# Layer 3 of a four-layer graph kernel: other tile shapes on TensorE, the key turn read from SBUF, and a new planned order

## The chip, the cores and the metric

The kernel runs on one core of a Trainium2 chip. The metric is the device time of one execution in microseconds; the kernel before is given as the median of three runs. A core has five engines that work side by side: TensorE (PE, matrix products; its weight loads are shown apart as PEld), VectorE (DVE), ScalarE (ACT), GpSimd (POOL) and SyncE (SP, which only issues DMAs). Matrix products land in PSUM, which ACT and DVE read; everything else lives in SBUF.

## The reference

Sixteen graphs (B = 16) of N = 1024 nodes with 128 features and a 0/1 adjacency matrix go through four layers. Each layer's result is added to its input, and a layer norm follows. Cut to what matters here:

```python
# layer 0: one head of additive attention, relu
# layer 1: eight heads of additive attention with 16 columns each, elu
# layer 2: mean over neighbours, product with a weight matrix, layer norm, relu
def _L3_gnn_ref(features, adj_matrix, W):               # layer 3
    D = W.shape[-1]                                     # 4 heads, D = 32
    Wh = jnp.einsum('bsf,hfd->bhsd', features, W)
    scores = jnp.einsum('bhsd,bhtd->bhst', Wh, Wh) / jnp.sqrt(jnp.float32(D))
    scores = jnp.where(adj_matrix[:, None, :, :] > 0, scores, NEG_INF)
    attn = jax.nn.softmax(scores, axis=-1)
    h = jnp.einsum('bhst,bhtd->bhsd', attn, Wh)
    ...
x = _layernorm(x + _L0_gnn_ref(x, adj, ...), axis=-1)
x = _layernorm(x + _L1_gnn_ref(x, adj, adj, ...), axis=-1)
x = _layernorm(x + _L2_gnn_ref(x, adj, ...), axis=-1)
x = _layernorm(x + _L3_gnn_ref(x, adj, ...), axis=-1)
```

## The kernel before

The kernel does not write its instructions in program order. It describes every graph as a list of steps, and a planner (class `Plan`) decides the order in which they are issued. A step has an engine, an estimated cost in microseconds, a due time, the buffers it reads and writes, and a function that issues its instructions. The planner keeps a clock for each engine from these estimates; among the open steps that could start first on an engine it takes the one with the earliest due time, and only those due within `AHEAD` of the oldest unfinished step. `LAG` and `SLACK` are added to the time at which a result counts as ready. `SWITCH` is added to a PE step whose `mode` differs from the one before. Each engine then runs its own list strictly in that order, and semaphores carry the dependences. So an estimate or a due time changes nothing by itself; it changes the order.

Buffers come from named pools. PSUM has two `wk` tiles of 128 x 1024 (two banks each), two `acc1` tiles and two `acc3` tiles of 128 x 512. SBUF pools bear on it too: nine `z` tiles (layer 1's weights), four `z3` tiles (layer 3's weights), six `gap` tiles, seven `R` tiles, and `m`, the adjacency in one byte, for three graphs.

The steps that matter, by graph:

- Layer 0 (`layer0`): DVE makes weights at L622, PE sums them at L634 into `acc1`.
- Layer 1 (`layer1`): for two groups of four heads and eight blocks j of 128 nodes, DVE makes four weight tiles of 128 x 1024 at L774, and PE sums them at L782, as two steps of four matmuls with 32 columns each, into `acc1`. The sums of weights come from a column of ones that stands in `hh1` beside each head's 16 values. ACT copies out at L812.
- Layer 2 (`layer2`): PE products with the adjacency at L914.
- Before layer 3 (`before3`), for each of two chunks of 512 nodes: transposes, the product with W at L991 into one half of a `wk` tile, a copy to `whT` at L995, the turn of the keys by seven small ACT copies at L1004 and L1006 (so that head h's 32 rows meet the right columns), transposes of the result into the other half of the same `wk` tile, and a copy to `hh` at L1018.
- Layer 3 (`layer3`), for two halves of 512 query nodes and eight blocks j of key nodes: ACT makes `gap` (L1060), zero at an edge and one elsewhere. One PE step makes the scores of all four heads in both `wk` tiles: at L1070 sixteen bf16 matmuls in 32x32 tiles put a large negative number where there is no edge, and at L1080 four fp32 matmuls, one for each head's 32 rows and 128 columns, add the products. ACT takes the exp of each `wk` tile into `z3` (L1113). Two PE steps at L1092 sum the weights into `acc3`, with two matmuls of 64 columns each: 32 values, one column of ones, and 31 zeros. `LATER3` sets how much later than the scores these steps are due.

Layer norms run on ACT (L426, L454), with small DVE steps and a power on POOL (L442). Due times come from the calls at the end of the function, once for each graph, `PERIOD` apart; graphs overlap, so that one graph's layer 1 stands beside the layer 3 of the graph before it.

The SP queue issues the loads of `x`, `xT` and `R` and the stores; POOL's queue issues the loads of `m` between its powers and reductions.

Of the kernel before, what the change touches and what calls it, by code (L numbers as in the profile page):

```python
# [76 lines left out]
class Plan:  # L77
# [6 lines left out]
    SLACK = 0.00  # L84
    SWITCH = 0.1
    SAME = 0.0
    AHEAD = 327.0

    def __init__(self):
        self.steps = []  # L90
        self.places = {}
        self.users = {}
        self.turns = {}

# [8 lines left out]
    def step(self, engine, us, due, emit, reads=(), writes=(), lag=None, holds=(), floor=0.0, mode="full"):  # L103
        s = Step(engine, us, due, emit, self.LAG if lag is None else lag, mode)
        s.ready = floor
        for buf in holds:
            s.bufs.append(buf)
            buf.left += 1
        follows = set()
        for keys, writing in ((reads, False), (writes, True)):  # L110
            for key in keys:
                buf, part = key if isinstance(key, tuple) else (key, None)
                if buf not in s.bufs:
                    s.bufs.append(buf)
                    buf.left += 1
                buf.parts.setdefault(part, [None, []])
                for p, (writer, readers) in buf.parts.items():
                    if part is None or p is None or p == part:
                        if writer:
                            follows.add(writer)  # L120
                        if writing:
                            follows.update(readers)
        for keys, writing in ((reads, False), (writes, True)):
            for key in keys:
                buf, part = key if isinstance(key, tuple) else (key, None)
                if writing:
                    for p in list(buf.parts):
                        if part is None or p == part:
                            buf.parts[p] = [s, []]
                else:  # L130
                    buf.parts[part][1].append(s)
        follows.discard(s)
        s.waits = len(follows)
        for f in follows:
            f.next.append(s)
        self.steps.append(s)
        return s
# [83 lines left out]
def tile_binary(  # L221
# [32 lines left out]
    W3 = D3 + 1  # L254
    F8 = mybir.dt.float8e5
    PAD1 = 32 - W1
    PAD3 = 64 - W3
# [14 lines left out]
    nc.gpsimd.memset(neg_half, -0.5)  # L272
    neg_one = const.tile([P, 1], F32, name="neg_one")
# [13 lines left out]
    LATER1 = 3.4  # L287
    LATER3 = 13.7
# [27 lines left out]

    plan.pool("wk", wks)
# [25 lines left out]
    for t in places("hh3", 3, [P, HB, H3 * W3 + PAD3]):  # L343
        nc.vector.memset(t[:, :, : H3 * W3].rearrange("p k (h c) -> p k h c", c=W3)[:, :, :, D3:], 1.0)
        nc.vector.memset(t[:, :, H3 * W3 :], 0.0)
# [191 lines left out]
    def before0(b, due):  # L537
# [11 lines left out]
        for chunk in range(2):  # L549
# [8 lines left out]
            ps, view = products(xT, w0c, due, hd, 0.93)  # L558
# [121 lines left out]
    def before1(b, due):  # L680
# [8 lines left out]
        for chunk in range(2):  # L689
            ks = slice(chunk * HB, (chunk + 1) * HB)  # L690
            xT = turned(x1, chunk, due + chunk)
            ps, view = products(xT, w1c, due + chunk, hh, 1.0)
# [169 lines left out]
    def layer2(b, due):  # L862
# [7 lines left out]
        for chunk in range(2):  # L870
            ks = slice(chunk * HB, (chunk + 1) * HB)
            xT = turned(x2, chunk, due + chunk)
            ps, view = products(xT, w2c, due + chunk, y2, 1.76)
# [101 lines left out]
    def before3(b, due):  # L975
# [6 lines left out]

        def heads(hh):
            return hh.t[:, :, : H3 * W3].rearrange("p k (h c) -> p k h c", c=W3)[:, :, :, :D3]

        for chunk in range(2):
# [5 lines left out]
                [xT, w3c], [(ps, 0)], holds=[hh, whT, turn],  # L992
# [3 lines left out]
                [(ps, 0)], [whT],  # L996
            )

            def turned_groups(turn=turn, ps=ps):
                for h in range(H3):  # L1000
                    rows_h = slice(h * D3, (h + 1) * D3)
                    into = blocks_of(turn.t[rows_h, :])
                    of = blocks_of(ps.t[rows_h, :HALF])
                    nc.scalar.copy(into[:, :, h * D3 :], of[:, :, : P - h * D3])  # L1004
                    if h:
                        nc.scalar.copy(into[:, :, : h * D3], of[:, :, P - h * D3 :])  # L1006

            step("ACT", 2.6, due + chunk, turned_groups, [(ps, 0)], [turn])
            step(
                "PE", 0.44, due + chunk,  # L1010
                lambda turn=turn, ps=ps: transposes(
                    ps.t[:, HALF:], [turn.t[:, k * P : (k + 1) * P] for k in range(HB)]
                ),
                [turn], [(ps, 1)],
# [3 lines left out]
                lambda hh=hh, ps=ps: nc.scalar.copy(  # L1018
                    heads(hh), ps.t[:, HALF:].rearrange("p (k h d) -> p k h d", k=HB, h=H3)
                ),  # L1020
                [(ps, 1)], [hh],
# [5 lines left out]
        for n, hh in enumerate(hhs):  # L1027
            step(
                "ACT", 0.48, due,
                lambda n=n, hh=hh: nc.scalar.activation(  # L1030
                    sq.t.rearrange("p (c k h d) -> p c k h d", c=2, k=HB, h=H3)[:, n], heads(hh), AF.Square
                ),
                [hh], [(sq, n)],
            )
# [14 lines left out]
    def layer3(b, due, span):  # L1049
# [3 lines left out]
        for half in range(2):  # L1053
# [10 lines left out]
            def scores(j, gap, sc, whT=whTs[half]):  # L1064
# [13 lines left out]
                for h in range(H3):  # L1078
                    rows_h = slice(h * D3, (h + 1) * D3)
                    nc.tensor.matmul(  # L1080
                        sc[h // 2].t[:, (h % 2) * HALF : (h % 2 + 1) * HALF],
                        lhsT=turns[j // HB].t[rows_h, j % HB * P : (j % HB + 1) * P],
                        rhs=whT.t[rows_h, :],
                        start=False,
                        stop=True,
                        skip_group_check=True,
                    )

            def weighted(j, g, z, av=av):
                for h in range(2):  # L1090
                    at = W3 * (2 * g + h)
                    nc.tensor.matmul(  # L1092
                        av[g].t[64 * h : 64 * h + 64, :],
                        lhsT=hhs[j // HB].t[:, j % HB, at : at + 64],
                        rhs=z.t[:, h, :],
                        start=j == 0,
                        stop=j == NB - 1,
                    )

            for j in range(NB):  # L1100
# [6 lines left out]
                    "PE", 1.34, at, lambda j=j, gap=gap, sc=sc, f=scores: f(j, gap, sc),  # L1107
# [65 lines left out]
    PERIOD = 133.3  # L1173
    weights(-190)
    for b in range(B):
        at = b * PERIOD
        at0 = 32 if b == 1 else at
        before0(b, at0 - 51)
        layer0(b, at0)
        before1(b, at - 77)  # L1180
        layer1(b, at + 83, 128)
        last1(b, at + 212)
        layer2(b, at + 223)
        before3(b, at + 199)
        layer3(b, at + 301, 141)
# [628 lines left out]
```

## Time and profile before

| | us |
|---|---|
| median of three runs | 2352.94 |
| lowest, highest | 2351.17, 2356.36 |
| profiled execution | 2357.02 |
| its span, first to last instruction | 2355.2 |
| PE busy | 2144.1 |
| DVE busy | 1875.7 |
| ACT busy | 1707.9 |
| POOL busy | 286.7 |
| L1080, busy | 295.8 |
| L1092, busy | 546.9 |
| L782, busy | 517.3 |
| L1113 (exp), busy | 542.6 |
| L774, busy | 1249.8 |

The profile shows one execution. A busy time is the time in which at least one such instruction ran. Matmuls overlap and their ends are modelled, so the distance from the start of one PE step to the start of the next says more than the mean of one matmul. An fp32 matmul leaves two records, so L1092 stands with 2048 records for 1024 matmuls. "Idle before" is the time an engine stood still just before an instruction, with what ended the wait. In the slices, each digit is the busy share of a fortieth of the span in tenths.

### The profile page before, as it was taken

The numbers are of one execution on the slowest core, as the hardware profiler recorded it, in microseconds if no ns is written. First come the engines' busy times: TensorE is split into PE (matmuls) and PEld (weight loads), VectorE is DVE, ScalarE is ACT, GpSimd is POOL, SyncE is SP. The second block draws the span as 40 slices with busy tenths as digits, with TensorE's granted clock in tenths as the row PEclk, the third lists the DMA queues.
The fourth block names the chain that finished last, engine by engine and source line by source line (L and its number), as shares of the span: only waits on it lengthen the run. The fifth ranks groups of instructions, "written<-read, shape, count | busy, mean of one in ns | idle before, by whom it ended". The sixth has DMA issues, their size and how long they took to land.

```text
span 2355.2 us, 47149 instructions
## 1 busy us (share of the span) xinstructions
PE 2144.1 (91%) x19376; PEld 996.5 (42%) x19376; DVE 1875.7 (80%) x2616; ACT 1707.9 (73%) x4214; POOL 286.7 (12%) x268
## 2 busy tenths in 40 slices
PE   5758899999999999999999999999999999998776
PEld 5515354443625445352534444363544436242321
DVE  4899888979797988979797897979789797995201
ACT  3414669698786969788686869868686987869675
POOL 2001011111011111111011111101111110110000
PEclk8879999999999999999999999999999999999988
DMA  6222221313122221312232131313213031200000
GB/s 103 57 65 32 82 37 52 72 24 87 32 82 37 83 40 24 87 41 78 33 95 31 33 92 24 84 26 97 32 57 66 14 87 24 73 10 10 1 10 11
DMA packets 80817, 119.32 MB, mean 51 GB/s; under 512 B 7384, under 2 KB 58704, under 8 KB 80592
## 3 DMA queue, kind: packets, MB, share of 16 engines
q1 hardware_dynamic: 62160, 99.43, 13.1%
q0 software_dynamic: 18432, 16.79, 8.7%
q8 instruction: 154, 2.52, 0.4%
q14 instruction: 71, 0.58, 0.1%
HBM read 157.55 MB, written 8.97 MB: 71 GB/s over the span
## 4 chain that ended last, share of the span: by engine, by line
PE 52%; DVE 24%; ACT 19%; issue 2%; POOL 1%; DMA 1%; POOLq 0%; DVEq 0%; ACTq 0%
PE acc L1092 15%; DVE z L774 13%; PE acc L782 10%; PE wk L1080 7%; PE acc L634 7%; ACT z L1113 5%; ACT junk L426 4%; PE wk L371 4%; PE wk L362 3%; ACT x L454 3%; PE wk L1070 2%; ACT turn L1004 2%; PE wk L914 2%; DVE tot L401 2%; DVE x L935 1%
## 5 line engine op out<-in xcount | busy, mean ns | idle before, releaser
L774 DVE SCALAR_TENSOR_TENSOR z<-R,q,m 128x1024 f32<-128x1024 f32 x1024 | 1249.8, 1278 | 53.2 <-PE acc L782 45.4
L1092 PE MATMUL acc<-z,hh 128*64 128x512 f32 x2048 | 546.9, 621 | 70.8 <-ACT z L1113 70.8
L1113 ACT ACTIVATE z<-wk,low 128x1024 f32<-128x1024 f32 x512 | 542.6, 1105 | 74.4 <-PE wk L1080 74.4
L782 PE MATMUL acc<-z,hh 128*32 128x512 f32 x4096 | 517.3, 615 | 60.6 <-DVE z L774 58.0
L426 ACT ACTIVATE junk<-x,off 128x128 f32<-128x128 f32 x640 | 257.3, 402 | 302.6 <-DVE off L420 286.0
L442 POOL TENSOR_TENSOR rstd<-rstd,b_neg_half 128x8 f32<-128x8 f32 (+1 forms) x81 | 176.1, 2174 | 1308.1 <-DVE rstd L437 1192.2
L1080 PE MATMUL wk<-whT,turn 32*128 32x512 f32 x2048 | 295.8, 647 | 0.0
L454 ACT ACTIVATE x<-x,shift,rstd 128x128 f32<-128x128 f32 x640 | 256.5, 488 | 31.7 <-DVE shift L448 31.7
L1092 PEld LDWEIGHTS acc<-z,hh 128*64 128x64 f32 x2048 | 106.4, 136 | 393.8 <-ACT z L1113 196.0
L634 PEld LDWEIGHTS acc<-hd,z 128*128 128x128 f32 x2048 | 243.6, 195 | 67.0 <-issue 18.5
L782 PEld LDWEIGHTS acc<-z,hh 128*32 128x32 f32 x4096 | 103.6, 110 | 389.5 <-issue 205.9
L634 PE MATMUL acc<-hd,z 128*128 128x129 f32 x2048 | 259.9, 282 | 7.0 <-DVE z L622 3.8
L914 PEld LDWEIGHTS <-m 128*128 128x128 fp8e5 x3072 | 178.6, 98 | 16.9 <-issue 16.8
L914 PE MATMUL wk<-y,m 128*128 128x128 bf16 (+1 forms) x3072 | 181.7, 220 | 3.6 <-DVE y L900 1.3
L1060 ACT ACTIVATE gap<-m,neg_one 128x512 bf16<-128x512 fp8e5 x256 | 183.6, 720 | 0.0
L622 DVE SCALAR_TENSOR_TENSOR z<-R,q,m 128x512 f32<-128x512 f32 x240 | 164.8, 745 | 4.6 <-DMA R<-rows 4.6
L1070 PEld LDWEIGHTS <-far 32*32 32x32 bf16 x4096 | 36.1, 88 | 209.1 <-issue 207.2
L1070 PE MATMUL wk<-gap,far 32*32 32x512 bf16 x4096 | 115.4, 388 | 6.8 <-ACT z L1113 2.9
L426 ACT ACTIVATION_READ_ACCUMULATOR junk<-x,off 128x1 f32 x640 | 120.6, 188 | 0.0
L1080 PEld LDWEIGHTS wk<-whT,turn 32*128 32x128 f32 x2048 | 80.8, 185 | 59.2 <-issue 59.2
L543 POOL DMA_DIRECT2D m<-in_adj_dram x128 | 73.0, 577 | 222.1 <-ACT gap L1060 205.9
L951 DVE TENSOR_TENSOR x<-x,b_gamma_bc 128x1024 f32<-128x1024 f32 x16 | 19.6, 1225 | 91.2 <-ACT x L454 91.2
(114 smaller groups left out, 1729.9 us busy)
## 6 DMA issues: line engine op xcount, KB each, us to landing
R<-rows SPq DMA_DIRECT2D x139, 512.0 KB
m<-in_adj_dram POOLq DMA_DIRECT2D x128, 128.0 KB, 4.4
xT<-in_xT_dram SPq DMA_DIRECT2D x32, 256.0 KB
x<-in_x_dram SPq DMA_DIRECT2D x16, 512.0 KB
out_dram<-x SPq DMA_DIRECT2D x15, 512.0 KB
rows<-rT SPq DMA_DIRECT2D x16, 32.0 KB
out_dram<-x SPq DMA_DIRECT2D x2, 256.0 KB
z<-in_L_gnn_a_dram SPq DMA_DIRECT2D x2, 128.0 KB
```

Of the source, the lines that this page charges most:

```text
L426: nc.scalar.activation(junk.t, y.t[:, k, :], AF.Square, bias=off.t[:, k : k + 1], accum_out=squared.t[:, k : k + 1])
L442: lambda: nc.gpsimd.tensor_tensor(rstd.t[:, ks], rstd.t[:, ks], neg_half[:, ks], ALU.pow),
L454: nc.scalar.activation(y.t[:, k, :], y.t[:, k, :], AF.Identity, bias=shift.t[:, k : k + 1], scale=rstd.t[:, k : k + 1])
L634: nc.tensor.matmul(av[k // 2].t.rearrange("p (k c) -> p k c", k=2)[:, k % 2, : P + 1], lhsT=z.t[:, at : at + P], rhs=hd.t[:, j, : P + 1], ...
L774: nc.vector.scalar_tensor_tensor(z.t, in0=G["R"][h].t, scalar=q.t[:, j, h : h + 1], in1=m[j].t, op0=ALU.max, op1=ALU.mult)
L782: nc.tensor.matmul(av[half].t[32 * c : 32 * c + 32, :], lhsT=hh.t[:, j, at : at + 32], rhs=zs[c].t[:, half * HALF : (half + 1) * HALF], st ...
L914: nc.tensor.matmul(ps.t[:, k * SLOT : k * SLOT + part.stop - part.start], lhsT=m[j].t[:, rows_i], rhs=y2.t[:, j, part], start=j == 0 and n ...
L1060: nc.scalar.activation(gap.t, m[j].t[:, cols], AF.Square, bias=neg_one, accum_out=squares[:, at : at + 1], saturate=False)
L1070: nc.tensor.matmul(sc[h // 2].t[c * 32 : (c + 1) * 32, (h % 2) * HALF : (h % 2 + 1) * HALF], lhsT=far[rows_r, rows_r], rhs=gap.t[rows_r, : ...
L1080: nc.tensor.matmul(sc[h // 2].t[:, (h % 2) * HALF : (h % 2 + 1) * HALF], lhsT=turns[j // HB].t[rows_h, j % HB * P : (j % HB + 1) * P], rhs ...
L1092: nc.tensor.matmul(av[g].t[64 * h : 64 * h + 64, :], lhsT=hhs[j // HB].t[:, j % HB, at : at + 64], rhs=z.t[:, h, :], start=j == 0, stop=j ...
L1113: lambda g=g, sc=sc, zs=zs: nc.scalar.activation(zs[g].t.rearrange("p h n -> p (h n)"), sc[g].t, AF.Exp, bias=low.t, scale=S3),
```

## The change

The scores matmuls at L1080 become eight of 32 rows and 64 columns; the order is by column half, then by head. The weighted sums at L1092 become four matmuls of 32 columns a step: two with the values of a head and two with a constant tile of ones, so the sums of weights come in 32 equal rows in place of one; the step's mode takes the name that layer 1's L782 has. `hh` loses its ones and zeros and becomes dense. In `before3`, the seven turn copies read `whT` in SBUF and not PSUM, as four steps in place of one, and the transposes get a `wk` tile of their own.

In the planner, `SLACK` goes from 0.00 to 0.05, `AHEAD` from 327 to 2741, and a new rule takes 79.6 us off the due time of each ACT or DVE step that touches `wk`, `acc1` or `acc3`. The estimates of some steps, `LATER1`, `LATER3`, `PERIOD` and the due times of all stages get other values.

```diff
-    SLACK = 0.00
+    SLACK = 0.05
...
-    AHEAD = 327.0
+    URGENT = 79.6
+    AHEAD = 2741.0
...
+        if engine in ("ACT", "DVE") and any(buf.pool in self.scarce for buf in s.bufs):
+            s.due -= self.URGENT
...
+    ones = const.tile([P, D3], F32, name="ones")
+    nc.vector.memset(ones, 1.0)
...
-    LATER1 = 3.4
-    LATER3 = 13.7
+    LATER1 = 0.6
+    LATER3 = 32.1
...
+    plan.scarce = ("wk", "acc1", "acc3")
...
-    for t in places("hh3", 3, [P, HB, H3 * W3 + PAD3]):
...
+    places("hh3", 3, [P, HB, H3 * D3])
...
-            def turned_groups(turn=turn, ps=ps):
-                for h in range(H3):
-                    rows_h = slice(h * D3, (h + 1) * D3)
-                    into = blocks_of(turn.t[rows_h, :])
-                    of = blocks_of(ps.t[rows_h, :HALF])
-                    nc.scalar.copy(into[:, :, h * D3 :], of[:, :, : P - h * D3])
-                    if h:
-                        nc.scalar.copy(into[:, :, : h * D3], of[:, :, P - h * D3 :])
-
-            step("ACT", 2.6, due + chunk, turned_groups, [(ps, 0)], [turn])
+            def turned_groups(h, turn=turn, whT=whT):
+                rows_h = slice(h * D3, (h + 1) * D3)
+                into, of = blocks_of(turn.t[rows_h, :]), blocks_of(whT.t[rows_h, :])
+                nc.scalar.copy(into[:, :, h * D3 :], of[:, :, : P - h * D3])
+                if h:
+                    nc.scalar.copy(into[:, :, : h * D3], of[:, :, P - h * D3 :])
+
+            pt = Buf("wk", "pt")
+            for h in range(H3):
+                step("ACT", 0.7 if h else 0.5, due + chunk, lambda h=h, f=turned_groups: f(h), [whT], [(turn, h)])
...
-                for h in range(H3):
-                    rows_h = slice(h * D3, (h + 1) * D3)
-                    nc.tensor.matmul(
-                        sc[h // 2].t[:, (h % 2) * HALF : (h % 2 + 1) * HALF],
-                        lhsT=turns[j // HB].t[rows_h, j % HB * P : (j % HB + 1) * P],
...
+                for r in range(2):
+                    for h in range(H3):
+                        rows_h = slice(h * D3, (h + 1) * D3)
+                        nc.tensor.matmul(
+                            sc[h // 2].t[r * 64 : (r + 1) * 64, (h % 2) * HALF : (h % 2 + 1) * HALF],
+                            lhsT=turns[j // HB].t[rows_h, j % HB * P + r * 64 : j % HB * P + (r + 1) * 64],
...
                 for h in range(2):
-                    at = W3 * (2 * g + h)
-                    nc.tensor.matmul(
-                        av[g].t[64 * h : 64 * h + 64, :],
-                        lhsT=hhs[j // HB].t[:, j % HB, at : at + 64],
...
+                    at = D3 * (2 * g + h)
+                    for n, lhsT in enumerate((hhs[j // HB].t[:, j % HB, at : at + D3], ones)):
+                        at = 64 * h + 32 * n
+                        nc.tensor.matmul(
+                            av[g].t[at : at + 32, :],
+                            lhsT=lhsT,
...
-                    "PE", 1.34, at, lambda j=j, gap=gap, sc=sc, f=scores: f(j, gap, sc),
+                    "PE", 1.23, at, lambda j=j, gap=gap, sc=sc, f=scores: f(j, gap, sc),
...
-                        "PE", 0.91, at + LATER3, lambda j=j, g=g, z=zs[g], f=weighted: f(j, g, z),
-                        [zs[g], hhs[j // HB]], [av[g]], mode="64 columns",
+                        "PE", 0.87, at + LATER3, lambda j=j, g=g, z=zs[g], f=weighted: f(j, g, z),
+                        [zs[g], hhs[j // HB]], [av[g]], mode="32 columns",
...
-    PERIOD = 133.3
-    weights(-190)
+    PERIOD = 126.2
+    weights(-185)
     for b in range(B):
         at = b * PERIOD
-        at0 = 32 if b == 1 else at
-        before0(b, at0 - 51)
+        at0 = 41 if b == 1 else at
+        before0(b, at0 - 45)
         layer0(b, at0)
-        before1(b, at - 77)
-        layer1(b, at + 83, 128)
-        last1(b, at + 212)
-        layer2(b, at + 223)
-        before3(b, at + 199)
-        layer3(b, at + 301, 141)
+        before1(b, at + 39)
+        layer1(b, at + 97, 116)
+        last1(b, at + 140)
+        layer2(b, at + 159)
+        before3(b, at + 220)
+        layer3(b, at + 317, 109)
```

More of the change, by code (lines that the diff above doesn't have):

```diff
@@ L93, in __init__ @@
         self.turns = {}
+        self.scarce = ()
     def pool(self, name, tiles):
@@ L253, in tile_binary @@
     W1 = D1 + 1
-    W3 = D3 + 1
     F8 = mybir.dt.float8e5
     PAD1 = 32 - W1
-    PAD3 = 64 - W3
     const = ctx.enter_context(tc.tile_pool(name="bconst", bufs=1))
@@ L342, in tile_binary @@
         nc.vector.memset(t[:, :, H1 * W1 :], 0.0)
-    for t in places("hh3", 3, [P, HB, H3 * W3 + PAD3]):
-        nc.vector.memset(t[:, :, : H3 * W3].rearrange("p k (h c) -> p k h c", c=W3)[:, :, :, D3:], 1.0)
-        nc.vector.memset(t[:, :, H3 * W3 :], 0.0)
+    places("hh3", 3, [P, HB, H3 * D3])
     for t in places("y2", 1, [P, NB, 3 * P + 2], BF16):
@@ L557, in before0 @@
             )
-            ps, view = products(xT, w0c, due, hd, 0.93)
+            ps, view = products(xT, w0c, due, hd, 1.2)
             step(
@@ L691, in before1 @@
             xT = turned(x1, chunk, due + chunk)
-            ps, view = products(xT, w1c, due + chunk, hh, 1.0)
+            ps, view = products(xT, w1c, due + chunk, hh, 1.08)
             step(
@@ L872, in layer2 @@
             xT = turned(x2, chunk, due + chunk)
-            ps, view = products(xT, w2c, due + chunk, y2, 1.76)
+            ps, view = products(xT, w2c, due + chunk, y2, 1.83)
             rest = Buf("rest", "rest")
@@ L981, in before3 @@
         turns = G["turn"] = [Buf("turn", f"turn_{b}_{n}") for n in range(2)]
-        def heads(hh):
-            return hh.t[:, :, : H3 * W3].rearrange("p k (h c) -> p k h c", c=W3)[:, :, :, :D3]
         for chunk in range(2):
@@ L991, in before3 @@
                 lambda xT=xT, ps=ps: nc.tensor.matmul(ps.t[:, :HALF], lhsT=w3c.t, rhs=xT.t, start=True, stop=True),
-                [xT, w3c], [(ps, 0)], holds=[hh, whT, turn],
+                [xT, w3c], [ps], holds=[hh, whT, turn],
             )
@@ L995, in before3 @@
                 "ACT", 0.48, due + chunk, lambda whT=whT, ps=ps: nc.scalar.copy(whT.t, ps.t[:, :HALF]),
-                [(ps, 0)], [whT],
+                [ps], [whT],
             )
-            def turned_groups(turn=turn, ps=ps):
-                for h in range(H3):
-                    rows_h = slice(h * D3, (h + 1) * D3)
-                    into = blocks_of(turn.t[rows_h, :])
-                    of = blocks_of(ps.t[rows_h, :HALF])
-                    nc.scalar.copy(into[:, :, h * D3 :], of[:, :, : P - h * D3])
-                    if h:
-                        nc.scalar.copy(into[:, :, : h * D3], of[:, :, P - h * D3 :])
-            step("ACT", 2.6, due + chunk, turned_groups, [(ps, 0)], [turn])
+            def turned_groups(h, turn=turn, whT=whT):
[7 more added lines that the diff above has]
+                step("ACT", 0.7 if h else 0.5, due + chunk, lambda h=h, f=turned_groups: f(h), [whT], [(turn, h)])
             step(
                 "PE", 0.44, due + chunk,
[L1011 to L1014, printed above, removed]
+                lambda turn=turn, pt=pt: transposes(pt.t, [turn.t[:, k * P : (k + 1) * P] for k in range(HB)]),
+                [turn], [pt],
             )
@@ L1017, in before3 @@
                 "ACT", 0.48, due + chunk,
[L1018 to L1021, printed above, removed]
+                lambda hh=hh, pt=pt: nc.scalar.copy(hh.t.rearrange("p k c -> p (k c)"), pt.t[:, :HALF]),
+                [pt], [hh],
             )
@@ L1030, in before3 @@
                 lambda n=n, hh=hh: nc.scalar.activation(
-                    sq.t.rearrange("p (c k h d) -> p c k h d", c=2, k=HB, h=H3)[:, n], heads(hh), AF.Square
+                    sq.t[:, n * HALF : (n + 1) * HALF], hh.t.rearrange("p k c -> p (k c)"), AF.Square
                 ),
@@ L1077, in scores @@
                         )
-                for h in range(H3):
-                    rows_h = slice(h * D3, (h + 1) * D3)
-                    nc.tensor.matmul(
-                        sc[h // 2].t[:, (h % 2) * HALF : (h % 2 + 1) * HALF],
-                        lhsT=turns[j // HB].t[rows_h, j % HB * P : (j % HB + 1) * P],
[L1083 to L1087, printed above, removed]
+                for r in range(2):
[4 more added lines that the diff above has]
+                            lhsT=turns[j // HB].t[rows_h, j % HB * P + r * 64 : j % HB * P + (r + 1) * 64],
+                            rhs=whT.t[rows_h, :],
+                            start=False,
+                            stop=True,
+                            skip_group_check=True,
+                        )
             def weighted(j, g, z, av=av):
                 for h in range(2):
-                    at = W3 * (2 * g + h)
-                    nc.tensor.matmul(
-                        av[g].t[64 * h : 64 * h + 64, :],
-                        lhsT=hhs[j // HB].t[:, j % HB, at : at + 64],
[L1095 to L1098, printed above, removed]
+                    at = D3 * (2 * g + h)
[4 more added lines that the diff above has]
+                            lhsT=lhsT,
+                            rhs=z.t[:, h, :],
+                            start=j == 0,
+                            stop=j == NB - 1,
+                        )
             for j in range(NB):
```

## The prediction

> **What bounds the kernel now.** I read the page's busy shares and slices first, then busy time by stretch, then the TensorE timeline of one graph, then the waits.
>
> ```profile
> PE 2144.1 (91%) x19376; PEld 996.5 (42%) x19376; DVE 1875.7 (80%) x2616; ACT 1707.9 (73%) x4214; POOL 286.7 (12%) x268
> PE   5758899999999999999999999999999999998776
> DVE  4899888979797988979797897979789797995201
> ```
>
> TensorE (PE) is full from the sixth slice to the fourth last; VectorE (DVE) is fuller only in the first slices, and the end has neither full. The stretches say the same in microseconds (columns: stretch, its length, then busy time of PE, PEld, DVE, ACT, POOL; granted clock; DMA):
>
> ```profile
> 120.00:180.00 60.00, 32.94 (x199) 8.21 (x197) 59.83 (x58) 12.72 (x41) 6.02 (x7) 0.80 0.23 60
> 435.00:570.00 135.00, 130.36 (x1222) 60.64 (x1206) 116.88 (x163) 106.06 (x264) 17.63 (x16) 1.00 0.24 56
> 2230.00:2290.00 60.00, 41.18 (x284) 12.06 (x276) 4.96 (x14) 45.74 (x101) 3.71 (x3) 0.83 0.04 9
> ```
>
> From 300 to about 2050 us the pattern repeats every 135.0 us, one graph each, 13 periods: PE 130.4 busy and 4.6 idle, DVE 18.1 idle, ACT 28.9 idle. Before 300 us DVE is the bound (59.83 of 60); after 2050 us the last graphs' chain is. So a saving counts in full where it is taken from PE in the 13 periods.
>
> The timeline gives what a step costs. Steps follow each other without a gap unless a bracket stands behind, so a price is the distance from one start to the next:
>
> ```profile
> 1006.26 2.78 PE L782 MATMUL acc<-z,hh 128*32 128x512 f32 x24
> 1008.97 0.43 PE L1070 MATMUL wk<-gap,far 32*32 32x512 bf16 x16
> 1009.34 1.14 PE L1080 MATMUL wk<-whT,turn 32*128 32x512 f32 x8
> 1010.41 1.07 PE L782 MATMUL acc<-z,hh 128*32 128x512 f32 x8
> 1012.37 1.08 PE L1092 MATMUL acc<-z,hh 128*64 128x512 f32 x4 [0.90 <-ACT z L1113]
> 1013.38 0.43 PE L1070 MATMUL wk<-gap,far 32*32 32x512 bf16 x16
> ...
> 1032.10 1.94 PE L1092 MATMUL acc<-z,hh 128*64 128x512 f32 x8
> 1033.96 1.09 PE L362 MATMUL wk<-b_ident,oT 128*128 128x128 f32 x8
> ...
> 1061.12 1.06 PE L782 MATMUL acc<-z,hh 128*32 128x512 f32 x8
> 1062.12 1.08 PE L1092 MATMUL acc<-z,hh 128*64 128x512 f32 x4
> ```
>
> An fp32 matmul leaves two records, so x8 on L782 is one step of four matmuls. One L782 step takes 1.00 (1061.12 to 1062.12), three take 2.71 (1006.26 to 1008.97): 0.86 a step and 0.14 for entering. One L1092 step takes 1.01 (1012.37 to 1013.38), two 1.86 (1032.10 to 1033.96): 0.86 and 0.15. Four 32-column tiles with 128 rows cost what two 64-column tiles cost; the entry is what a change of tile shape costs. A scores step is 0.37 (L1070) and 1.07 (L1080).
>
> The waits of PE from 300 to 2050 us add up to 66.3; the two largest:
>
> ```profile
> PE acc L1092 <- ACT z L1113: 42.3, 49, 1.2
> PE acc L782 <- DVE z L774: 10.0, 13, 1.3
> ```
>
> **The change, part by part.** All counts are from the instruction order of the two built programs.
>
> *Values and sums in 32 columns.* Before, L1092 sends two 64-wide matmuls a step; after, four 32-wide ones (two against the new tile of ones). By the L782 row the step itself still costs 0.86: nothing. But it now has the tile shape of layer 1's L782, so a step beside an L782 step has no entry. In a steady graph, the stream has 18 runs of L782 and 28 of L1092 before, and 29 joint runs after: 18 x 0.14 + 28 x 0.15 = 6.7 against 29 x 0.14 = 4.0, **2.7 saved a graph**. If entering costs 0.15 still: 2.4.
>
> *Scores in 32x64.* L1080 goes from four 32x128 matmuls to eight 32x64. No row shows fp32 in this shape. The nearest: a lone step costs 1.07 with 128 columns (L1080), 1.01 with 64 (L1092), 1.00 with 32 (L782); weight loads are 185, 136 and 110 ns. That the eight run together is shown in parts: L1070 runs sixteen 32x32 tiles in 0.37, L1080 four row strips, L782 four column strips. Bounds: 1.00 from L782; above, if only four run at a time, one more pass of 0.86 (the slow rival). I take 1.02, nearest to the 64-wide row with a little for more tiles: 0.05 x 16 = **0.8 a graph**. The trace's fp32 records of one step start 7 ns apart, so four more tiles are 0.03 us by the row. The Trainium skill, "TensorE: Matmul & The Clock Gate", section "Measured speedup vs the span model", puts about 4 ns on each further tile, so 0.02; over 256 steps the two differ by under 3 us.
>
> *Order.* Runs of L634 fall from 8 to 5 a graph; one step 0.99, two 1.98, three 2.78, so about 0.1 for entering: 0.3 saved. L991 is split into two runs: 0.1 lost. **Net 0.2.**
>
> *Stalls.* What waits at L1092 is the in-order PE queue: L782, L1070 and all else behind it; then DVE for z tiles and ACT for scores. Adding up PE work between the end of a scores step and its first weighted step gives 2.6 us on average before, 7.6 after. Two exps of 1.1 stand there. In a steady graph 9 of 16 have 2.0 us or less before, 2 of 16 after. Scaled, 42.3 x 2/9 = 9; the other 24 I leave: 33 in place of 66, **2.5 saved a graph** in 13. Bounds: nothing saved, as the distance to the next scores step (needs both wk tiles) stays at 6.5 and 6.4 us; or all but 15 gone, 4 a graph. What is late next is DVE: 116.9 of about 129.
>
> *Keys turned from SBUF, separate pt tile.* The seven copies a chunk now read whT, not PSUM. Rows: 2.74 us a chunk now; a 128x512 copy from PSUM takes 587 ns (L995), a cast from SBUF 619 (L895): about 30 ns more, 7 copies x 32 chunks = 7 us on ACT, covered by its 28.9 idle a graph. If that cover were gone it would be 0.4 a graph. The wk tile that was held over the turn, the transposes and the copy (2.7 + 0.6 + 0.6, twice a graph, in which no scores step can start, as it needs both) is now free after one copy of 0.59, and a second is taken for the transposes; what that gives is in the stalls.
>
> *PSUM's last users first.* ACT and DVE steps on wk, acc1 or acc3 overtake layernorms and gap tiles. ACT's gap (L1060, 0.72 and 0.20) is needed by scores 8 us later by due time; between a graph's stages the PE queue has 37 to 66 us of other work after, 33 to 64 before, which covers a later layernorm. Nothing. The SP queue has the same 707 rows, loads of R and x in another order; DVE's wait for R is 3.8 us at L774 and 4.6 at L622 in all, so nothing. POOL's rows fall from 763 to 735 by merging alone; its m loads wait for gap (205.9 us in all), and no PE row waits for m.
>
> "TensorEngine Tiling (Array Packing)", section "PSUM Bottleneck" in the Trainium skill, speaks against: faster tiles may leave PSUM evacuation as the bound. The evacuation here is ACT, 106.1 busy of 135.0; at 129 it is 82%. By the rule nothing would be gained; the row leaves room.
>
> *Sum.* PE 130.4 - 2.7 - 0.8 - 0.2 = 126.7 a graph; idle 4.6 falls by 2.5; period 135.0 - 3.7 - 2.5 = 128.8; 13 x 6.2 = 81. Head: DVE-bound, its work unchanged, 0 (bounds: 10 lost by the moved layers, 10 gained). Tail: 32 scores x 0.05 and some entries, 3. Together 84 from the profiled 2357.0 (span 2355.2 and 1.8 around it): 2273. The median of the runs, 2352.9, lies 4 lower: **2269**.
>
> **Rivals.**
> - *The work shrinks, the stalls don't* (they move from the exp to the wk tiles or DVE's z). For: the unchanged 6.4 us to the next scores step. Against: the tripled distance. 3.7 x 13 + 3 = 51: **2302**.
> - *Stalls go almost fully, the head gains too.* Idle falls by 4.0: 7.7 x 13 + 3 + 10 = 113: **2240**. For: the wk tile is held for less. Against: DVE would be at 92%.
> - *DVE becomes the bound.* It waits 18.1 a graph, mostly not for PE (L774 for L782: 45 us in all); if these waits are fixed by its queue's order, the period stays 135: **2350**. Against: PE waited for z only 10 us in 13 graphs.
> - *Slower: eight fp32 tiles don't run together.* A scores step becomes 1.88, 0.81 more: 13.0 a graph, less 2.9 for entries and order and 2.5 for stalls, 7.6 x 13 = 99, and 26 in the tail: **2478**. Against: the sixteen bf16 tiles. It decides once a scores step costs 0.33 more than I take (84 / 256), a pitch of 1.35.
>
> **How the numbers follow.** Forecast 0.52, stalls stay 0.23, more gained 0.14, DVE-bound 0.06, slower 0.05. The range takes in the first three with the bounds (low: the third case with scores at 1.00, 0.3 x 13 = 4 less; high: entries at 0.15, scores at 1.07 and no stall gone leave 2.6 x 13 = 34, and 10 lost in the head): 2236 to 2329. Two tenths of a per cent, 5 us, is about what a measurement tells. DVE-bound splits between faster, the same and slower: faster 0.91, same 0.03, slower 0.06.
>
> **What would show it.** Period of about 129 us; PE busy near 127 a period; the scores matmul's pitch 1.02; joined runs of layer 1 and layer 3 matmuls without the 0.14; waits for the exp under 15 us from 300 to 2050. Wrong if the pitch of scores is above 1.07, if PE's idle stays at 4.6 or over, or if DVE is over 95% busy in a period.

## The result, and the profile after

The changed kernel is slower: 2364.85 us median of five runs (2363.18 to 2366.69) against 2352.94 for the kernel before in the same comparison (2349.41 to 2356.36), a ratio of 1.005 with a 95% interval of 1.0035 to 1.0065. The forecast was 2269 and the range ended at 2329. The profiled execution has a span of 2363.0 us. Its page:

```profile
span 2363.0 us, 55375 instructions
PE 2121.8 (90%) x23472; PEld 981.6 (42%) x23472; DVE 1863.1 (79%) x2611; ACT 1711.2 (72%) x4214; POOL 295.3 (12%) x268
PE   4858799898998989999998999899899999999876
L785 PE MATMUL acc<-z,hh 128*32 128x512 f32 x4096 | 537.2, 637 | 112.9 <-DVE z L777 111.8
```

PE has less to do than before (2121.8 busy against 2144.1) and takes longer. Its slices, which read 9 almost without a break, now have 8s among them. L785 is layer 1's weighted sum, L782 before; L777 the DVE line that makes its weights. The waits of PE from 300 to 2050 us (total, times, longest):

```profile
PE acc L785 <- DVE z L777: 62.1, 12, 5.9
PE wk L917 <- ACT z L1112: 14.2, 13, 1.2
PE acc L1091 <- ACT z L1112: 4.5, 14, 1.4
```

The wait for the exp at layer 3's weighted sum has gone from 42.3 to 4.5, as forecast. A wait that was 10.0 before, for layer 1's weights from DVE, is 62.1: twelve times about 5.2 us, once a graph. The count and the longest tell the two kinds apart: before, 49 small waits for the exp; now, 12 large ones for the weights. The wait at L917, layer 2's product, is for the exp too.

The period is measured between the starts of layer 2 of graphs 2 and 12, ten periods. Busy time by stretch, of after and then of before (length, then PE, PEld, DVE, ACT, POOL; granted clock; DMA):

```profile
467.10:1832.50 1365.40, 1294.68 (x14621) 601.79 (x14621) 1163.24 (x1623) 1063.06 (x2631) 187.49 (x160) 0.97 0.24 55
```

```profile
454.90:1807.60 1352.70, 1303.87 (x12064) 606.39 (x12060) 1169.38 (x1621) 1061.13 (x2630) 179.81 (x160) 1.00 0.25 56
```

A period was 135.3 us with 130.4 of PE work; it is 136.5 with 129.5. The work shrank by 0.9 where 3.7 was forecast, and the granted clock fell from 1.00 to 0.97, which makes the same work longer.

That the steps themselves became cheaper is seen where nothing disturbs them. The PE timeline of after, start to start:

```profile
1075.56 0.43 PE L1065 MATMUL wk<-gap,far 32*32 32x512 bf16 x16
1075.93 1.11 PE L1076 MATMUL wk<-whT,turn 32*64 32x512 f32 x16
1076.97 1.92 PE L785 MATMUL acc<-z,hh 128*32 128x512 f32 x16
1078.83 0.66 PE L365 MATMUL wk<-b_ident,turn 128*128 128x128 f32 x4
```

The eight fp32 matmuls of 32x64 take 1.04 (1075.93 to 1076.97); four of 32x128 took 1.07. They run together.

What fails is seen by following the stall back, engine by engine. PE, with one period's stall (a run of L1065 and lines of L1091 left out):

```profile
1116.20 1.90 PE L785 MATMUL acc<-z,hh 128*32 128x512 f32 x16
...
1119.25 1.11 PE L1076 MATMUL wk<-whT,turn 32*64 32x512 f32 x16
1125.54 3.64 PE L785 MATMUL acc<-z,hh 128*32 128x512 f32 x16 [5.17 <-DVE z L777]
```

DVE at that time:

```profile
1111.76 0.16 DVE L440 TENSOR_SCALAR rstd<-squared 128x8 f32<-128x8 f32 x1
...
1112.11 3.67 DVE L777 SCALAR_TENSOR_TENSOR z<-R,q,m 128x1024 f32<-128x1024 f32 x3
1121.73 0.17 DVE L451 TENSOR_TENSOR shift<-off,rstd 128x8 f32<-128x8 f32 x1 [5.96 <-POOL rstd L445]
1121.82 4.87 DVE L777 SCALAR_TENSOR_TENSOR z<-R,q,m 128x1024 f32<-128x1024 f32 x4
```

POOL at that time:

```profile
1105.71 1.25 POOL L397 PARTITION_ALL_REDUCE all<-top  x1 [13.59 <-DVE top L578]
1111.65 0.74 POOL L546 DMA_DIRECT2D m<-in_adj_dram  x1 [4.68 <-ACT gap L1055]
1120.02 1.68 POOL L445 TENSOR_TENSOR rstd<-rstd,b_neg_half 128x8 f32<-128x8 f32 x1 [7.63 <-issue]
```

Read them from the bottom. POOL finishes layer 0's reduction over partitions at 1106.96. Next in its queue is a load of `m`, which waits 4.68 us until ACT's `gap` has read the old `m`. Behind that stands a layer norm's power. Its input is there at 1111.92 (L440), the load is issued by 1112.39, and yet the power starts at 1120.02: 7.63 us that the timeline puts to "issue", to nothing it shows. The view of line L445 has what the timeline leaves out, two commands to POOL at 1112.5, right behind the load:

```profile
L445 POOLq MODIFY_POOL_CONFIG  x2: 37/37/37, 1112.5 to 1112.5; - x2
```

Such a pair stands in the queue wherever POOL goes from a reduction to a power, and another where it goes back. This text calls it a change of code. DVE has come to the step that reads this power, a `shift` of 0.17 us, and waits 5.96. This `shift` belongs to the last layer norm of the graph before, on which only a store hangs; but DVE is in order, and the next four weights of layer 1 (L777) stand behind it. PE runs out of them and stands 5.17 us. Then it works at half clock: the granted clock is 0.50 from 1124.2 (the last 1.3 us of the stop) to 1131.0, and the L785 group that took 1.90 takes 3.64.

### The profile page after: what moved, and what is told of

Its sections match the earlier page's. It is cut to its first block, busy times and chain, and to the rows that moved or that the text cites. A ratio compares the mean times of both kernels' runs of the same rounds, so it can differ in the third digit from the quotient of the medians.

```text
span 2363.0 us, 55375 instructions
## 1 busy us (share of the span) xinstructions
PE 2121.8 (90%) x23472; PEld 981.6 (42%) x23472; DVE 1863.1 (79%) x2611; ACT 1711.2 (72%) x4214; POOL 295.3 (12%) x268
## 3 DMA queue, kind: packets, MB, share of 16 engines
q1 hardware_dynamic: 62160, 99.43, 12.3%
## 4 chain that ended last, share of the span: by engine, by line
PE 70%; DVE 15%; ACT 8%; issue 5%; POOL 1%; DMA 0%; POOLq 0%; DVEq 0%; ACTq 0%
PE acc L785 17%; PE acc L1091 14%; DVE z L777 10%; PE acc L637 9%; PE wk L1076 8%; PE wk L917 8%; PE wk L365 5%; PE wk L374 5%; ACT z L1112 3%; PE wk L1065 3%; ACT junk L429 1%; PE wk L990 1%; POOL rstd L445 1%; DVE tot L404 1%; ACT x L457 1%
## 5 line engine op out<-in xcount | busy, mean ns | idle before, releaser
L777 DVE SCALAR_TENSOR_TENSOR z<-R,q,m 128x1024 f32<-128x1024 f32 x1024 | 1247.6, 1277 | 2.7 <-DMA R<-rows 1.5
L785 PE MATMUL acc<-z,hh 128*32 128x512 f32 x4096 | 537.2, 637 | 112.9 <-DVE z L777 111.8
L1091 PE MATMUL acc<-z,hh 128*32 128x512 f32 x2048 | 526.1, 612 | 30.3 <-ACT z L1112 30.2
L1091 PE MATMUL acc<-z,ones 128*32 128x512 f32 x2048 | 526.0, 612 | 0.0
L429 ACT ACTIVATE junk<-x,off 128x128 f32<-128x128 f32 x640 | 256.8, 401 | 221.1 <-DVE off L423 205.9
L445 POOL TENSOR_TENSOR rstd<-rstd,b_neg_half 128x8 f32<-128x8 f32 (+1 forms) x81 | 171.6, 2118 | 1193.2 <-DVE rstd L440 1068.4
L1076 PE MATMUL wk<-whT,turn 32*64 32x512 f32 x4096 | 290.0, 623 | 0.0
L785 PEld LDWEIGHTS acc<-z,hh 128*32 128x32 f32 x4096 | 111.7, 113 | 420.9 <-issue 238.0
L637 PEld LDWEIGHTS acc<-hd,z 128*128 128x128 f32 x2048 | 235.2, 192 | 44.4 <-ACT x L658 14.6
L637 PE MATMUL acc<-hd,z 128*128 128x129 f32 x2048 | 245.3, 277 | 4.0 <-ACT x L658 2.9
L1091 PEld LDWEIGHTS acc<-z,hh 128*32 128x32 f32 x2048 | 102.5, 111 | 274.8 <-issue 196.7
L917 PE MATMUL wk<-y,m 128*128 128x128 bf16 (+1 forms) x3072 | 183.3, 221 | 18.0 <-ACT z L1112 16.8
L917 PEld LDWEIGHTS <-m 128*128 128x128 fp8e5 x3072 | 181.7, 98 | 31.1 <-issue 31.1
L1091 PEld LDWEIGHTS acc<-z,ones 128*32 128x32 f32 x2048 | 102.3, 111 | 77.9 <-issue 77.9
L1065 PE MATMUL wk<-gap,far 32*32 32x512 bf16 x4096 | 119.3, 390 | 7.5 <-DVE x L834 4.2
L1065 PEld LDWEIGHTS <-far 32*32 32x32 bf16 x4096 | 36.8, 88 | 210.2 <-issue 205.5
```

What stands on the lines that cost most here:

```text
L429: nc.scalar.activation(junk.t, y.t[:, k, :], AF.Square, bias=off.t[:, k : k + 1], accum_out=squared.t[:, k : k + 1])
L445: lambda: nc.gpsimd.tensor_tensor(rstd.t[:, ks], rstd.t[:, ks], neg_half[:, ks], ALU.pow),
L637: nc.tensor.matmul(av[k // 2].t.rearrange("p (k c) -> p k c", k=2)[:, k % 2, : P + 1], lhsT=z.t[:, at : at + P], rhs=hd.t[:, j, : P + 1], ...
L777: nc.vector.scalar_tensor_tensor(z.t, in0=G["R"][h].t, scalar=q.t[:, j, h : h + 1], in1=m[j].t, op0=ALU.max, op1=ALU.mult)
L785: nc.tensor.matmul(av[half].t[32 * c : 32 * c + 32, :], lhsT=hh.t[:, j, at : at + 32], rhs=zs[c].t[:, half * HALF : (half + 1) * HALF], st ...
L917: nc.tensor.matmul(ps.t[:, k * SLOT : k * SLOT + part.stop - part.start], lhsT=m[j].t[:, rows_i], rhs=y2.t[:, j, part], start=j == 0 and n ...
```

## The experiments

The theory formed here: a power that follows a reduction on POOL has to wait some 7 to 10 us for POOL's change of code; with the load of `m` between the two, that change starts only behind the load's own wait, and so ends too late for DVE. The rivals: the waiting load alone is the cause; the new tile shapes are at fault; the due times of layer 1 simply put its weights too late on DVE.

### The load issued behind the power

```diff
+    def power(rstd, ks):
+        nc.gpsimd.tensor_tensor(rstd.t[:, ks], rstd.t[:, ks], neg_half[:, ks], ALU.pow)
+        last[0] = "power"
+        while held:
+            held.pop(0)()
...
+        if b >= 3 and last[0] == "reduce":
+            held.append(load)
+        else:
+            load()
```

> The changed kernel, with each load of m that the plan puts on POOL between a reduction and the next power issued behind that power; the other queues keep their order. Theory (POOL's queue): after the reduction POOL waits for a slot of m, only then starts the 7.5 us change of its code for the power, the power is 6 us late for DVE's shift, the z weights behind it are late for PE, PE stands 5.2 us and then runs at half clock for some 5 us. Then here the power ends near the time DVE asks for it, PE's wait for L777 from 300 to 2050 us falls from 62 to under 15, the granted clock there is 1.00, the period goes from 136.5 to about 128.6, and the time to 2262 (2250 to 2290). Rival (DVE is too full at this pace): the wait for z comes back at another place, PE still waits over 40 us, time 2340 to 2365.

Measured: 2320.47 us, ratio to before 0.9832 (0.981 to 0.9854). About half of the way from after to the expectation. The period is 132.35. POOL's timeline in this run:

```profile
957.04 1.25 POOL L404 PARTITION_ALL_REDUCE all<-top  x1 [13.59 <-DVE top L599]
968.32 1.68 POOL L398 TENSOR_TENSOR rstd<-rstd,b_neg_half 128x8 f32<-128x8 f32 x1 [10.03 <-issue]
969.98 0.74 POOL L409 DMA_DIRECT2D m<-in_adj_dram  x1
```

Nothing stands between the two now, and still 10.03 us pass. The load's wait was only a part: DVE waits 2.93 for the same `shift`, PE 2.15. So "the load alone" falls, and the expectation, which took the change of code to be hidden in full, was too low. Its pair of commands stands at 958.2, at the reduction's end, and the change took 10.03 us, not the 7.5 that the expectation had.

### The change of code ahead of the load

```diff
+    def reduced(got, v, op):
+        nc.gpsimd.partition_all_reduce(got.t, v.t, P, op)
+        if v.name == "top0":
+            nc.gpsimd.tensor_tensor(spare, one_neg, neg_half[:, :1], ALU.pow)
```

A spare power of one column, read by nobody, directly behind layer 0's reduction; the load of `m` stays ahead of the real power.

> The changed kernel with a power on one spare column put right behind layer 0's reduction, ahead of the load of m; m stays where it is. So POOL changes its code while it would have waited for m's slot. Theory (the change of code behind the wait is what is late, not the wait itself): the power comes some 3 to 4 us earlier, DVE's wait at the shift falls from 6.0 to 2 to 3 us, PE's wait to about 2 us a period with no drop of the clock, time 2275 to 2310. Rival (the wait for m alone delays the power): nothing changes, 2355 to 2370. Rival (DVE too full): 2340 to 2365.

Measured: 2337.44 us, 0.9905 (0.9882 to 0.9928): some 1% faster than before and 1.5% faster than after, and slower than expected. DVE's wait at the shift is 4.29 here and not 2 to 3, and the clock still drops. POOL's timeline:

```profile
1096.33 1.25 POOL L399 PARTITION_ALL_REDUCE all<-top  x1 [13.59 <-DVE top L586]
1107.62 0.59 POOL L401 TENSOR_TENSOR spare<-one_pos,b_neg_half 128x1 f32<-128x1 f32 x1 [10.04 <-issue]
1108.18 0.74 POOL L554 DMA_DIRECT2D m<-in_adj_dram  x1
1108.95 1.68 POOL L453 TENSOR_TENSOR rstd<-rstd,b_neg_half 128x8 f32<-128x8 f32 x1
```

This is the cleanest view of the cost. The spare power waits for no data and starts 10.04 us after the reduction's end; the real power, right behind the load, starts with no such gap. So the gap belongs to the first power behind a reduction, whichever power that is. It isn't the reduction running on, either: DVE reads the reduction's result at 1102.44, 5.2 us before the gap ends. And it comes the other way round too, before a reduction behind a power, as in the early graphs of after:

```profile
400.95 0.38 POOL L397 PARTITION_ALL_REDUCE all<-bound  x1 [6.33 <-issue]
428.59 0.38 POOL L397 PARTITION_ALL_REDUCE all<-top  x1 [9.16 <-issue]
```

The load's wait now lies beside it, and from the reduction to the power it is 11.4 us, where after has 13.1 and the run before this one 10.0.

### No reductions on POOL

```diff
-        step("POOL", 1.6, due, lambda: nc.gpsimd.partition_all_reduce(got.t, v.t, P, op), [v], [got], lag=0.6)
+        step("POOL", 1.6, due, lambda: nc.gpsimd.tensor_copy(got.t, v.t), [v], [got], lag=0.6)
```

The order of every queue stays; the maxima over partitions are left out, each partition keeps its own value. This kernel does not compute what the reference does; it shows only what the time would be.

> The changed kernel with every maximum over partitions on POOL replaced by a copy of each partition's own value, order kept. The kernel then leaves out these maxima (they only scale the exponents). POOL then never changes its code. Theory (the change of code, 7.5 to 10 us, is what is left of the loss after the load of m is moved): PE's wait for L777 goes from 62 to under 10 us between 300 and 2050 us, the clock stays at 1.00, the period is 128.5 to 130, time 2260 to 2285. Rival (DVE too full): period 132 or more as in the run with m moved, 2315 to 2330.

Measured: 2256.32 us, 0.9572 (0.9542 to 0.9601). POOL's timeline, and then busy time over ten periods:

```profile
1055.91 1.10 POOL L397 COPY all<-top 128x1 f32<-128x1 f32 x1 [13.76 <-DVE top L578]
1061.88 0.60 POOL L546 DMA_DIRECT2D m<-in_adj_dram  x1 [4.86 <-ACT gap L1055]
1062.51 2.64 POOL L445 TENSOR_TENSOR rstd<-rstd,b_neg_half 128x8 f32<-128x8 f32 x1
```

```profile
448.20:1736.40 1288.20, 1269.61 (x14620) 598.53 (x14620) 1161.54 (x1623) 1059.04 (x2631) 194.15 (x160) 1.00 0.25 59
```

The copy takes as long as the reduction did (1.10 against 1.25) and the load waits as long (4.86 against 4.68), but the power follows it at once. From 300 to 2050 us this run has no MODIFY_POOL_CONFIG at all, where after has 28 in front of powers and 28 in front of reductions. PE's wait for L777 falls from 62.1 to 1.8, the clock is 1.00 throughout, the period is 128.82 with 126.96 of PE work. So the load's wait costs nothing without the gap; due times of layer 1 are no cause; and DVE, at 116.2 of 128.8, does not bind.

The same edit in the kernel before shows whether that kernel paid for its own gaps.

> The same copy in place of the maxima in the kernel before (maxima left out). Theory: its PE waits for the exp, not for DVE, and its powers have their code changed early enough, so it gains little: 2335 to 2353. Rival (the change of code also holds the kernel before): 2300 to 2330, and its period falls by 2 us or more.

Measured: 2340.19 us, 0.9922 (0.9893 to 0.9951), a period of 134.77 in place of 135.28. Before had the gap too:

```profile
1051.67 0.67 POOL L394 PARTITION_ALL_REDUCE all<-bound  x1 [16.39 <-DVE bound L1038]
1052.86 1.33 POOL L394 PARTITION_ALL_REDUCE all<-top  x1 [0.52 <-DVE top L575]
1061.22 1.81 POOL L442 TENSOR_TENSOR rstd<-rstd,b_neg_half 128x8 f32<-128x8 f32 x1 [7.03 <-DVE z L774]
```

It is 7.03 us there, but no load stands in it, its first 4.9 us pass while the power's input is not yet made, and DVE has three weights of 3.67 us together to do meanwhile: its wait for the `shift` was 0.39. So most of it was covered: without its reductions the kernel before gains 0.5 us a period, and layer 2 of graph 2 starts 6.1 us earlier. Before even had nearly twice as many changes, 52 and 52 of these commands from 300 to 2050 us. Not their number but what stands behind them makes the loss; the new order took the cover away.

### Order alone, shapes alone

After's order with before's tile shapes: scores, weighted sums and `hh` of the change are taken back.

```diff
-                for r in range(2):
-                    for h in range(H3):
+                for h in range(H3):
...
-                    for n, lhsT in enumerate((hhs[j // HB].t[:, j % HB, at : at + D3], ones)):
...
+                        lhsT=hhs[j // HB].t[:, j % HB, at : at + 64],
```

> The changed kernel's order with the tile shapes of before: scores 32x128, values and ones in 64 columns. Theory (POOL's queue): the stall of PE and the drop of the clock stay, as the order makes them; PE work grows by 2.2 us a period (0.03 x 16 for scores, 12 more entries of 0.14), part of it in the time PE would have stood: 2365 to 2395. Rival (the new shapes make the loss): faster than the changed kernel, 2300 to 2350, with no stall for z.

Measured: 2386.9 us, 1.0115 (1.0092 to 1.0138); PE's wait for layer 1's weights is as in after:

```profile
PE acc L789 <- DVE z L781: 61.6, 13, 5.8
```

The shapes are not at fault, the order is. With the order given, the shapes gain: 1.0115 to before without them, 1.005 with them, some 15 us; the period 137.61 and 136.53.

Before's order with after's tile shapes: the same parts, put into the kernel before.

```diff
-                for h in range(H3):
+                for r in range(2):
+                    for h in range(H3):
...
-                        lhsT=hhs[j // HB].t[:, j % HB, at : at + 64],
...
+                    for n, lhsT in enumerate((hhs[j // HB].t[:, j % HB, at : at + D3], ones)):
```

> The kernel before, its order kept, with the new tile shapes alone (keys still turned from PSUM). The joint runs of L782 and the 32-column sums are 29 a graph in this order too, 17 fewer entries of 0.14, and scores are 0.03 shorter: 2.9 us less PE work a period, less what PE then waits longer for the exp. Theory: faster than before, 2310 to 2335. Rival (the new shapes make the loss): 2353 or slower.

Measured: 2349.03 us, 0.9944 (0.9925 to 0.9963). The expectation was missed. The two waits of PE for the exp, from 300 to 2000 us:

```profile
PE acc L1096 <- ACT z L1117: 53.7, 48, 1.8
PE wk L362 <- ACT z L1117: 17.4, 13, 1.9
```

PE has 2.1 us less work a period (128.31 against 130.39) and the period does not move (135.40 against 135.28). The waits for the exp, 41.7 and 4.2 before in the same stretch, take up most of it. The clock, 1.00 throughout before, was at 0.50 for 13.7 us of the ten periods. In before's order PE's work is not what sets the period; what does was not pinned down, only that it comes back to PE as a wait for the exp. So the prediction's premise that a saving on PE counts in full in the 13 periods does not hold in before's order. The gain that is left lies in the head and the tail.

### A version that beats both

If the reduction is the trouble, layer 0's maximum can be made without it: SP stores the 128 partial maxima to DRAM and loads them back into every partition, DVE takes the maximum. Added to the first experiment's edit:

```diff
+        step(
+            "SP", 0.5, due,
+            lambda: nc.sync.dma_start(out=kept.t.rearrange("(p c) -> p c", c=count), in_=v.t), [v], [kept], lag=2.5,
+        )
+        step(
+            "SP", 0.5, due, lambda: nc.sync.dma_start(out=every.t[:, : P * count], in_=kept.t.partition_broadcast(P)),
+            [kept], [every], lag=2.5,
+        )
+        step(
+            "DVE", 0.1 + 0.14 * count, due,
+            lambda: nc.vector.tensor_reduce(got.t, every.t[:, : P * count].rearrange("p (n c) -> p c n", c=count), AX.X, ALU.max),
...
```

> A version that computes the reference. The changed kernel with two edits: loads of m go behind the power as in the run before, and layer 0's maximum over partitions leaves POOL: the 128 values go to DRAM, come back on every partition, and DVE takes their maximum; planned as two DMA steps and one DVE step. The other two reductions of a graph then end some 20 us before the power that is needed next, so POOL has changed its code in time. Theory: PE's wait for the z weights from 300 to 2000 us under 15 us, clock 1.00, period 128.5 to 130.5, time 2255 to 2290, the fastest of all that compute the reference. Rival (DVE too full, or the DMA chain of some 6 us is late for layer 0): period over 132, 2315 or more.

Measured: 2315.53 us, 0.9832 (0.9815 to 0.9849), above the expectation. The period is 129.81, near that without reductions, but layer 2 of graph 2 starts at 492.5 us where after has 467.1: the way through DRAM is slow where the first graphs wait for it, and DVE waits 18.9 us for it in the first graph and 7.1 in the second. So in the second form only graphs from the fourth on take that way, and the planner is told 4.0 us for the load in place of 2.5:

```diff
-        if v.name != "top0":
+        if not by_dma:
...
-            [kept], [every], lag=2.5,
+            [kept], [every], lag=4.0,
...
+        most = over_partitions(top, bass_isa.ReduceOp.max, [P, 1], due, by_dma=b >= 3)
```

> A version that computes the reference. As the run before, but the maximum by DMA only from the fourth graph on, and its return planned 1.5 us later. In the run before, the steady period was 129.8 us, but the first graphs came 16 to 40 us later than in the changed kernel, as the small DMAs of graphs 0 to 2 stand behind the first large loads. Theory: the head is that of the changed kernel again (layer 2 of graph 2 starts near 467, not 492), the period stays at 129 to 130, time 2270 to 2290. Rival (the head is late for another reason): 2305 or more.

Measured: 2292.3 us, 0.9734 (0.9716 to 0.9752), just over the expectation and the best of the versions that compute what the reference does. The period is 130.18, and layer 2 of graph 2 starts at 471.4 us, so the head is nearly that of after again. PE's largest wait from 300 to 2050 us:

```profile
PE acc L825 <- DVE z L817: 24.6, 15, 3.3
```

The next thing in the way is probably the DRAM path itself: DVE waits 30.0 us for it in these 1750. No run takes it away alone.

### One row through all of them

The wait of DVE for the power at `shift`, and the period, of all versions with after's shapes and order (the two by DRAM have other steps, so the planner changed their order a little):

| version | DVE's wait at `shift`, 300 to 2050 us | period, us | clock below 1 in the same stretch, us |
|---|---|---|---|
| after | 73.7 | 136.5 | 88.8 |
| change of code ahead of the load | 50.3 | 133.7 | 58.0 |
| load behind the power | 37.6 | 132.4 | 30.7 |
| maximum by DRAM, later graphs | 4.4 | 130.2 | 17.1 |
| maximum by DRAM, all graphs | 4.1 | 129.8 | 20.5 |
| no reductions | 0 | 128.8 | 0 |

Period and wait fall together, and the clock's share with them, but for the last step between the two DRAM rows.

## Why the prediction was wrong, step by step

*Entries: right.* An L785 step takes 0.97 alone, two 1.86, so 0.09 for entering is not paid again, and L785 and L1091 run on without it. *Scores: right in kind, half in size.* 1.04, not 1.02: 0.4 us a graph in place of 0.8. With nothing in the way (no reductions) PE has 126.96 a period; the sum said 126.7. (One period was read as 135.0; over ten it is 135.28, with 4.9 idle and not 4.6.)

*Stalls at the exp: right; stalls in all: wrong.* L1092's wait goes from 42.3 to 4.5, where 9 was forecast. With L917's 14.2 and two small ones, all of PE's waits for the exp go from 49.7 to 22.9, not under the 15 that was named as a sign. With nothing in the way PE's idle time a period is 1.86, where the sum left 2.1. But in the changed kernel it is 7.07, above the 4.6 that the prediction itself called a sign of being wrong.

*Turn copies from SBUF: right.* The seven copies take 96.6 us over 32 chunks, 3.02 each, where 2.74 was read before: some 40 ns a copy, not 30, on an engine with time to spare.

*The period: right for a kernel that the change did not make.* 128.8 was forecast and 128.82 measured, but only without the reductions. That the two agree so closely is partly luck: PE's work is 0.26 more than the sum, its idle time 0.24 less.

*The step that failed* is the one on the order of POOL: "Nothing. ... POOL's rows fall from 763 to 735 by merging alone; its m loads wait for gap (205.9 us in all), and no PE row waits for m." The waits in it are read rightly, and the conclusion is wrong. It counted POOL's rows and asked who waits for the load's result. It did not ask what the load stands in front of in POOL's queue, nor who waits for that. The sentence on layer norms has the same hole: other work on PE "covers a later layernorm", but DVE, in order, stands at the late norm's `shift` with L777 behind it. A period is now reduction, load, power; the load's wait and then the change of code come ahead of the power; DVE waits at `shift`, and L777 waits behind it. The price, from after against the run without reductions: PE idle 7.07 a period against 1.86, so 5.2, and PE's work 129.46 against 126.96, so 2.5 for the half clock. Together 7.7, the whole of 136.53 - 128.82. That is more than the 6.2 that the forecast saved.

The profile of before could have told it. Its waits of POOL from 300 to 2050 us held this row:

```profile
POOL rstd L442 <- DVE z L774: 85.1, 12, 7.7
```

A power does not read layer 1's weights; its input comes from L437. A releaser that has nothing to do with the instruction means that the engine waited for something else: here the same 7 us behind a reduction, once a graph. It cost little where it stood, so it was read as nothing at all.

*Head and tail.* The sum put 0 on the head, with bounds of 10; layer 2 of graph 2 starts 12.3 us later than before, and 6.6 earlier without the reductions. Ten periods cost 12.6 more, and what follows them is 17.1 shorter. These three make the 7.8 between the two spans.

*The rivals.* "Eight fp32 tiles don't run together" and "DVE becomes the bound" both fell. The one in which "the work shrinks, the stalls don't" comes nearest: it names a move of the stalls to DVE's z, and there they are. But it priced them at what they were, where they grew and brought the half clock, and POOL is not in it. The slower side was looked for in the tiles, where the change's name is, and not in the queue that the new order rearranged.

## What to carry to other kernels

Where a new order puts an instruction that waits into an in-order queue, ask what stands behind it and who waits for that, on POOL and DVE too, however little they are used: an engine that is 12% busy cost this kernel 7.7 us of every 136.5. Look in the profile of before for idle time with a releaser that the instruction does not read, or with none, and keep what covers it today in view when the order changes. And keep POOL's reductions away from powers that an in-order engine will soon need, or make one of the two elsewhere.

## What the runs showed of the hardware

The change of code on POOL took 7.03 us in before, 7.63 in after (counted from the load) and 10.03 and 10.04 in the two runs where the load no longer stood between. Its two commands, MODIFY_POOL_CONFIG, take some 0.1 us; the rest of the gap has no record. It begins only when the queue has come that far: the commands stand at 1112.5 in after, behind the load, and at the reduction's end in the other three. Why its length differs stays open. The Trainium skill, "GPSIMD Engine Reference", section "2.1 Instruction dispatch", speaks of about 6 us (5.95) for the first call after a load of code, invisible in the profile; that these gaps are such a load is read from the commands at their start and from the experiments that move or remove them, and they are longer than the page's figure.

The clock is dear after a short stop. A PE wait of 5.17 us brought 6.8 us at a granted 0.50, and waits of 5.2 to 5.9 us did so in every steady period of after. With the load behind the power the wait is 2.15 and this stretch followed it:

```profile
974.90:978.30 3.40, 3.40 (x33) 0.57 (x24) 3.40 (x5) 1.29 (x4) 2.63 (x1) 0.50 0.29 96
```

PE is busy in all of it, at half clock; this came in five of the ten periods, and the L806 group at its start took 2.67 where 1.90 is usual. The Trainium skill, "TensorE: Matmul & The Clock Gate", section "HAM oscillation — how this bites in real kernels", puts the limit at idle gaps of about 3.4 us; here gaps of 2.10 to 2.76 were enough in five periods, while gaps of 2.35 to 2.77 in the five others left the clock at 1.00, so length alone does not decide below that limit. Where the gap falls decides too: from 300 to 2050 us all stretches at half clock of this run begin and end on one grid of 3.41 us. In the five periods with a drop the gap lay in one step of this grid, but for at most 0.15 us, and in the five others across two. Two such steps, the first with a drop behind it, the second without:

```profile
1633.66:1637.07 3.41, 1.31 (x20) 0.42 (x16) 3.41 (x3) 3.41 (x7) 0.00 (x0) 1.00 0.50 38
1104.58:1108.00 3.42, 1.39 (x16) 0.49 (x20) 3.42 (x5) 3.42 (x8) 0.07 (x1) 1.00 0.37 33
```

PE was busy for 0.65 to 1.31 us of the step ahead of the five drops, and for 1.39 or more in every step of the five other gaps. That is no sharp limit: with the shapes alone, gaps of 1.80 and 1.86 us brought a drop four times, and others as long did not. Before, whose longest PE wait from 300 to 2050 us was 1.8, was at 1.00 throughout.
